# Normalisation rows fetched from sixteen DRAM copies, and a new order for the first two batches

## The chip, the cores and the metric

One Trainium2 chip; the program uses a single NeuronCore with its engines: PE (TensorE, matmuls), DVE (VectorE), ACT (ScalarE), POOL (GpSimd) and SP (SyncE, which here only issues DMAs). The metric is the device time of one execution in microseconds (us), less is better.

## The reference

One layer of a graph network over 64 batches of 256 tokens with 768 features:

```python
h = jnp.maximum(_layernorm(x, axis=-1), 0.0)
deg, rdeg = adj.sum(-1), swapaxes(adj, 1, 2).sum(-1)      # degrees, at least 1 where they divide
ctx = adj @ (h @ Wadj.T + badj) / deg + adj.T @ (h @ Wrev.T + brev) / rdeg + h @ Wself.T + bself
rel = agg @ Wr.T + br * deg + ragg @ Wrr.T + brr * rdeg   # agg, ragg: sums of rows of E over the neighbours
x = x + ctx + rel
```

All of it is float32. The adjacency matrix holds zeros and ones.

## The kernel before

The product of `h` (2 token tiles of 128, in 6 feature tiles) with the three weight matrices is made by a bilinear scheme of 15 products in place of 18 (`PRODUCTS`); every operand is split into two parts, so that three fast passes on PE give float32 accuracy. Batches 1 to 62 go twice through the chip: sweep 1 (8 of the products) for all of them, then sweep 2 (7 products and the multiplication with the adjacency matrix). What sweep 1 makes is stored to DRAM ("kept") and loaded again for sweep 2. Batch 0 and batch 63 don't use the scheme: `whole` multiplies them with the weights directly, in 144 slower matmuls each, while the prepared weights ("words", three for each product, made by POOL, ACT and DVE from the raw weights) are being made for the sweep that follows. So the order of time is: an opening with filler matmuls on PE ("early", "late", made by `idle`), batch 0 through `whole`, sweep 1 from about 65 us to 1,100 us, batch 63 through `whole`, sweep 2.

In front of each batch (`front1`) the layer norm's statistics are taken from `x`, token by token (one token is one partition). The products want `h` transposed, tokens along the free axis, so the mean and the power of the variance must be rows that every partition can read. For batches 1 to 63 the four columns of statistics (two token tiles, mean and scale) stand in `cols`, 8 floats apart; DVE's `transpose` turns them into `line`, in blocks of 32 by 32; SP stores them to a DRAM tile `d` (512 floats), waits for that store, and loads `d` into all 128 partitions as `row`; POOL subtracts the mean row from the transposed `x` (`centre`, tile `h`), DVE scales (`norm`). Batch 0 uses PE instead ("place" on ACT, "spread" on PE, then centre and norm on DVE). `x` is then added a bias row and stored to DRAM ("keep c01", in the trace `kept<-x`), which sets its buffer of class B free for the next operands ("left").

No engine's order is written by hand: `record` gives every operation a cost and a rank (base rank plus the entry of its kind in the table `OFFSETS`; never below the ranks of what it depends on), and `Plan.schedule` runs through time with those costs, takes on each engine the operation of lowest rank that could start, and so fixes each engine's program. SP's DMAs are issued in that order too; an SP instruction that must wait holds up those behind it. In the kinds, `@` marks batch 0, `@1` batch 1, `$1` and `$` batches 62 and 63; a kind without a mark is that of the other batches or of a shared operation. Buffers are slots of classes (`SLOTS`); `line` was one of six slots of class S.

By their ranks the first transfers of before are x1 (-2209), x0 (-1451), raw00 (-659), raw20 (-376), xt0 (-360), the bias row adj (-282), raw02 (-257), xt1 (-214), raw10 (-100). An x, an xt (transposed x of one token tile) and a bias row have 384 KB, a raw (a third of one weight matrix) 768 KB.

Of the kernel before, what the change touches and what calls it, by code (L numbers as in the profile page):

```python
# [10 lines left out]
F32 = mybir.dt.float32  # L11
# [3 lines left out]
ALU = mybir.AluOpType  # L15
AX = mybir.AxisListType

P = 128
# [64 lines left out]
AHEAD = 5.0  # L83
PACE = 5.0
# [17 lines left out]
    "b2-a1": -115.71, "b2-a1$1": -26.76, "b2-a1@1": 24.4, "bias adj": -308.49, "bias forward": 38.92,  # L102
    "bias rev": 8.51, "bias rev again": 15.38, "bias reverse": 37.66, "bias self": 29.13, "bias self again": 10.67,
# [10 lines left out]
    "degree": 7.82, "degree$": -107.61, "degree$1": -68.79, "degree@": -10.26, "degree@1": -1.22, "double adj": 37.35,  # L114
    "double own": 12.97, "eT": 9.08, "early@": 52.17, "eps": -95.99, "eps$": 0.14, "eps$1": -7.48, "eps@": 47.5,
# [8 lines left out]
    "first 8$1": -96.9, "first 8@1": 22.79, "first 9": 10.11, "first 9$1": 12.79, "first 9@1": 11.63, "flag": 294.89,  # L124
# [301 lines left out]
def record(nc, plan, fixed, B, NREL, part=None):  # L426
    F, C, H = 6, 2, 768
# [261 lines left out]
    def front1(b):  # L689
# [47 lines left out]
        else:  # L737
# [5 lines left out]
            def spread():  # L743
                nc.sync.dma_start(
                    t(d).rearrange("k (q j) -> q k j", q=4), t(line).rearrange("(m e) j -> m e j", e=8)[:, 0]
                )
# [518 lines left out]
```

## Time and profile before

| what | value |
|---|---|
| time, median of 3 runs | 2431.03 us (2430.84 to 2432.28) |
| the profiled execution, its own time | 2432.28 us |
| its span, first to last instruction | 2432.2 us |
| PE busy | 2414.3 us, 99% |
| DVE, ACT, POOL busy | 2111.8 (87%), 2083.9 (86%), 1413.5 us (58%) |
| granted PE clock, mean | 0.998 of full speed |
| DMA traffic | 593.06 MB, mean 244 GB/s |

PE's busy time counts pipelined matmuls with modelled ends, so a stretch can read as fully busy and still hold fewer matmuls than another of the same length. The number of matmuls in a stretch, the `x` count, tells more.

### The profile page before, as it was taken

The numbers are of one execution on the slowest core, as the hardware profiler recorded it, in microseconds if no ns is written. First come the engines' busy times: TensorE is split into PE (matmuls) and PEld (weight loads), VectorE is DVE, ScalarE is ACT, GpSimd is POOL, SyncE is SP. The second block draws the span as 40 slices with busy tenths as digits, with TensorE's granted clock in tenths as the row PEclk, the third lists the DMA queues.
The fourth block names the chain that finished last, engine by engine and source line by source line (L and its number), as shares of the span: only waits on it lengthen the run. The fifth ranks groups of instructions, "written<-read, shape, count | busy, mean of one in ns | idle before, by whom it ended". The sixth has DMA issues, their size and how long they took to land.

```text
span 2432.2 us, 43543 instructions
## 1 busy us (share of the span) xinstructions
PE 2414.3 (99%) x13600; PEld 2356.8 (97%) x13600; DVE 2111.8 (87%) x3953; ACT 2083.9 (86%) x3934; POOL 1413.5 (58%) x1230
## 2 busy tenths in 40 slices
PE   9999999999999999999999999999999999999998
PEld 6999999999999999996999999999999999999998
DVE  6888898888988988875888888898888888888988
ACT  7888888888888888887988888888888888888887
POOL 7666566666666666665555555555555555555554
PEclk9999999999999999999999999999999999999999
DMA  7788888888788888877666666666666666666664
GB/s 275 248 271 283 267 283 279 271 278 270 268 285 273 273 282 275 282 248 253 222 221 221 221 222 221 222 223 223 221 221 221 221 221 221 221 222 221 224 223 154
DMA packets 225545, 593.06 MB, mean 244 GB/s; under 512 B 25116, under 2 KB 25116, under 8 KB 225308
## 3 DMA queue, kind: packets, MB, share of 16 engines
q1 hardware_dynamic: 225308, 590.22, 71.8%
q8 instruction: 109, 1.79, 0.3%
q14 instruction: 128, 1.05, 0.1%
HBM read 366.65 MB, written 223.48 MB: 243 GB/s over the span
## 4 chain that ended last, share of the span: by engine, by line
PE 96%; ACT 1%; DVE 1%; DMA 1%; issue 1%; POOL 0%; SPq 0%; ACTq 0%; DVEq 0%; POOLq 0%
PE x L599 21%; PE y L599 20%; PE agg L936 14%; PE w L599 10%; PE z L599 10%; PE v L599 5%; PE t L599 5%; PE u L599 5%; PE whole L806 4%; DMA kept<-x 1%; PE spread L719 1%; ACT agg L944 0%; DMA kept_h<-h 0%; DVE c L681 0%; ACT y L652 0%
## 5 line engine op out<-in xcount | busy, mean ns | idle before, releaser
L924 POOL TENSOR_TENSOR hl<-c,hl 128x768 fp32r<-128x768 f32 x256 | 471.8, 1854 | 544.9 <-ACT hl L920 298.6
L599 PE MATMUL x<-word,left 128*128 128x384 f32 x2976 | 577.3, 335 | 1.3 <-ACT x L652 0.9
L599 PE MATMUL y<-word,left 128*128 128x384 f32 x2976 | 570.0, 335 | 2.1 <-DVE c L665 0.8
L599 PEld LDWEIGHTS y<-word,left 128*128 128x128 f32 x2976 | 519.4, 188 | 7.2 <-ACT y L652 3.2
L599 PEld LDWEIGHTS x<-word,left 128*128 128x128 f32 x2976 | 519.1, 188 | 4.6 <-ACT x L652 1.2
L936 PE MATMUL agg<-hl,a 128*128 128x384 f32 x2048 | 398.6, 336 | 3.7 <-ACT agg L944 3.7
L936 PEld LDWEIGHTS agg<-hl,a 128*128 128x128 f32 x2048 | 359.9, 188 | 5.2 <-ACT agg L944 4.5
L765 POOL TENSOR_TENSOR h<-h,row 128x768 f32<-128x768 f32 x126 | 231.4, 1856 | 216.9 <-DMA h<-in_x_t_dram 82.8
L599 PE MATMUL w<-word,left 128*128 128x384 f32 x1488 | 300.7, 336 | 1.0 <-ACT c L670 0.7
L599 PE MATMUL z<-word,left 128*128 128x384 f32 x1488 | 299.3, 335 | 0.2 <-ACT z L652 0.2
L599 PEld LDWEIGHTS w<-word,left 128*128 128x128 f32 x1488 | 260.7, 188 | 5.8 <-ACT c L670 3.4
L599 PEld LDWEIGHTS z<-word,left 128*128 128x128 f32 x1488 | 258.0, 188 | 4.3 <-ACT c L670 0.5
L954 DVE SCALAR_TENSOR_TENSOR c<-agg,rd,c 128x768 f32<-128x768 f32 x252 | 254.5, 1010 | 3.0 <-PE agg L936 2.1
L920 ACT ACTIVATE hl<-c 128x768 fp32r<-128x768 f32 x256 | 213.8, 836 | 0.7 <-DVE c L681 0.5
L652 ACT ACTIVATE x<-x 128x768 f32<-128x768 f32 x248 | 191.4, 793 | 26.0 <-PE x L599 18.4
L652 ACT ACTIVATE y<-y 128x768 f32<-128x768 f32 x248 | 195.3, 787 | 4.0 <-PE y L599 1.6
L588 DVE SCALAR_TENSOR_TENSOR left<-left,top 128x256 fp32r<-128x256 f32 x496 | 188.9, 411 | 0.3
L944 ACT ACTIVATE agg<-row_forward,sqd 128x768 f32<-128x768 f32 x128 | 115.4, 902 | 85.6 <-DVE c L679 85.6
L588 DVE SCALAR_TENSOR_TENSOR left<-left 128x256 fp32r<-128x256 f32 x434 | 185.4, 438 | 0.1
L578 ACT ACTIVATE top<-left 128x256 f32<-128x256 f32 x496 | 176.4, 381 | 9.8 <-DVE left L588 8.8
L681 DVE SCALAR_TENSOR_TENSOR c<-x,c 128x768 f32<-128x768 f32 x124 | 118.2, 953 | 68.8 <-ACT agg L944 66.1
L769 DVE SCALAR_TENSOR_TENSOR h<-h,row 128x768 f32<-128x768 f32 x126 | 149.2, 1186 | 0.0
(131 smaller groups left out, 4631.7 us busy)
## 6 DMA issues: line engine op xcount, KB each, us to landing
c<-kept SPq DMA_DIRECT2D x316, 384.0 KB
kept<-c SPq DMA_DIRECT2D x252, 384.0 KB
x<-in_x_dram SPq DMA_DIRECT2D x128, 384.0 KB
h<-in_x_t_dram SPq DMA_DIRECT2D x128, 384.0 KB
out_dram<-c SPq DMA_DIRECT2D x126, 384.0 KB
kept_h<-h SPq DMA_DIRECT2D x124, 384.0 KB
h<-kept_h SPq DMA_DIRECT2D x124, 384.0 KB
adj<-in_adj_dram SPq DMA_DIRECT2D x64, 512.0 KB
```

The source lines that it names most:

```text
L578: lambda: nc.scalar.activation(view(top), t(w)[:, 0].bitcast(F32), AF.Copy),
L588: lambda: nc.vector.scalar_tensor_tensor(t(w)[:, 2], t(w)[:, 1].bitcast(F32), -STEP, first(), op0=ALU.mult, op1=ALU.add), s == 1,
L599: nc.tensor.matmul(t(q)[:, half, : H // 2], t(w)[:, lw, f, :], t(r[rw])[:, f, ts(half, H // 2)], start=start and i == 0 and f == 0, stop=s ...
L652: lambda: nc.scalar.activation(view(), view(), AF.Copy, scale=scale),
L681: emit = lambda to=to, sign=sign: nc.vector.scalar_tensor_tensor(to(), view(), sign * UP, to(), op0=ALU.mult, op1=ALU.add)
L765: lambda h=h, one=one, engine=engine: engine.tensor_tensor(t(h), t(h), one(0), op=ALU.subtract),
L769: lambda h=h, one=one: nc.vector.scalar_tensor_tensor(t(h), t(h), 0.0, one(1), op0=ALU.max, op1=ALU.mult), b != 0 or part is not None,
L920: lambda: nc.scalar.activation(t(pair)[:, 0], t(o), AF.Copy, scale=LOWER),
L924: lambda: nc.gpsimd.tensor_tensor(t(pair)[:, 1], t(o), t(pair)[:, 0].bitcast(F32), op=ALU.subtract),
L936: nc.tensor.matmul(t(q)[:, half, : H // 2], t(s["a"])[:, c, k, ts(ic, P)], t(pairs[c])[:, part, ts(half, H // 2)], start=False, stop=(c == ...
L944: lambda q=q, ic=ic, row=row: nc.scalar.activation(t(q)[:, :, : H // 2], t(row).rearrange("p (k n) -> p k n", k=2), AF.Copy, scale=t(sqd)[ ...
L954: lambda q=q, to=to, ic=ic: nc.vector.scalar_tensor_tensor(to(), t(q)[:, :, : H // 2], t(rd)[:, ic, k : k + 1], to(), op0=ALU.mult, op1=AL ...
```

## The change

It has three parts.

1. `line` is one tile of 128 by 128 for the whole kernel instead of a slot for each batch. One transpose of 128 by 32 becomes four of 32 by 32, whose results stand side by side: `line` has the four statistics in partitions 0, 8, 16 and 24, 128 floats each. The planner's cost stays 0.17. (At the end `flag` uses the same tile for its scratch.)
2. `d` has sixteen copies of the 512 floats: the store writes 64 pieces of 512 bytes instead of 16 of 128, and `row` lets partitions 0 to 7 read the first copy, 8 to 15 the second, and so on. Before, all 128 partitions read the same 2 KB.
3. `OFFSETS` gets other entries for 216 kinds: those of batch 0 (57), batch 1 (95) and the words and loads of the opening; the entries of all other batches stay. `idle`'s counts of filler matmuls stay too.

```diff
+COPIES = 16
...
-            line = plan.buf("S", [P, 32], F32, f"line_{b}")
-            dve(0.17, r - 19.5, f"line {b}", [col], [line], lambda: nc.vector.transpose(t(line), t(col)))
-            d = plan.buf(None, None, None, "d", v["dram"].tile([4, P], F32, tag="d", name=f"d_{b}"))
+            line = v["line"]
+            def turn():
+                for q in range(4):
+                    nc.vector.transpose(t(line)[:32, ts(q, 32)], t(col)[ts(q, 32), :])
+            dve(0.17, r - 19.5, f"line {b}", [col], [line], turn)
+            d = plan.buf(None, None, None, "d", v["dram"].tile([COPIES, 4, P], F32, tag="d", name=f"d_{b}"))
...
-                    t(d).rearrange("k (q j) -> q k j", q=4), t(line).rearrange("(m e) j -> m e j", e=8)[:, 0]
+                    t(d).rearrange("r k p -> k r p"),
+                    t(line)[:32].rearrange("(k e) p -> k e p", e=8)[:, 0].unsqueeze(1).to_broadcast([4, COPIES, P]),
...
-                    t(row).rearrange("p k i -> p (k i)"), t(d).rearrange("k p -> (k p)").partition_broadcast(P)
+                    t(row).rearrange("p k i -> p (k i)"), t(d).rearrange("r k p -> r (k p)").unsqueeze(1).to_broadcast([COPIES, P // COPIES, 4 * P]),
...
-        rest = plan.buf("S", [P, B, C], F32, "rest")
+        rest = v["line"]
...
+            "line": own("line", [P, P], F32),
```

Of `OFFSETS`, the entries that the prediction speaks of, with the rank that follows (base rank plus entry) in brackets:

| kind | before | after |
|---|---|---|
| load raw00.0 | -673.18 (-659) | -1386.44 (-1372) |
| x1@, x0@ | -2208.17, -1448.79 (-2209, -1451) | -724.49, -711.01 (-725, -713) |
| load raw20.0 | -389.67 (-376) | -718.11 (-704) |
| xt1@ | -222.9 (-214) | -683.93 (-675) |
| load raw02.0 | -286.41 (-257) | -100.61 (-71) |
| bias adj | -308.49 (-282) | -96.49 (-70) |
| load raw10.0 | -113.7 (-100) | -23.35 (-9) |
| xt0@ | -367.66 (-360) | 15.05 (23) |
| write10@, write00@ | -1521.37, -590.36 (never below bias adj) | -37.41, 2.12 (-5, 27) |
| centre1@, centre0@ | -452.7, -6.79 | 44.54, 27.55 |
| early@, late@ | 52.17, 74.89 | 303.01, 51.7 |


## Rows read from the trace of the kernel before

**Rows 1.** The page, part 1: busy time, share of the span, instructions of each engine.

```profile
PE 2414.3 (99%) x13600; PEld 2356.8 (97%) x13600; DVE 2111.8 (87%) x3953; ACT 2083.9 (86%) x3934; POOL 1413.5 (58%) x1230
```

**Rows 2.** Windows of PE: length, PE busy (matmuls), granted clock, DMA share, GB/s.

```profile
100.00:1000.00 900.00, 899.38 (x5162) 1.00 0.83 276
1250.00:2150.00 900.00, 899.93 (x5184) 1.00 0.65 222
```

**Rows 3.** Timeline of PE, 0 to 80 us: start, length, what.

```profile
12.15 1.03 PE L732 MATMUL spread<-spread 128*128 128x256 f32 x4
13.02 2.17 PE L719 MATMUL spread<-ident 128*128 128x128 f32 x18
17.27 48.32 PE L806 MATMUL whole<-raw,h 128*128 128x384 f32 x144 [2.08 <-issue]
...
73.41 0.97 PE L599 MATMUL y<-word,left 128*128 128x384 f32 x4 [0.76 <-DVE c L665]
...
75.26 1.68 PE L599 MATMUL y<-word,left 128*128 128x384 f32 x8 [0.17 <-ACT y L652]
```

**Rows 4.** Windows of PE in the opening; the columns of rows 2.

```profile
65.60:75.30 9.70, 8.53 (x45) 1.00 0.65 230
```

**Rows 5.** Windows of the `whole` matmuls of batch 0 alone; the columns of rows 2.

```profile
17.27:21.77 4.50, 4.50 (x9) 0.63 1.03 401
21.77:65.70 43.93, 43.82 (x136) 1.00 0.71 250
```

**Rows 6.** Timelines of DVE, ACT and POOL, 0 to 32 us.

```profile
4.96 0.96 DVE L704 BATCH_NORM_STATS2 stats<-x 128x6 f32<-128x384 f32 x2
...
15.23 0.95 DVE L765 TENSOR_TENSOR h<-h,spread 128x768 f32<-128x768 f32 x1 [8.85 <-PE spread L719]
16.22 0.95 DVE L769 SCALAR_TENSOR_TENSOR h<-h,spread 128x768 f32<-128x768 f32 x1
...
7.27 0.98 ACT L726 ACTIVATE spread<-ident,cols 128x128 f32<-128x128 f32 x3 [0.60 <-POOL cols L712]
13.24 1.55 ACT L609 ACTIVATE whole<-row_adj 128x768 f32<-128x768 f32 x2 [4.98 <-DMA row_adj<-in_bias_dram]
...
11.08 3.58 POOL L497 TENSOR_TENSOR right<-raw,raw 128x768 f32<-128x768 f32 x2 [3.85 <-DMA raw<-in_Wadj_dram]
15.31 3.59 POOL L497 TENSOR_TENSOR right<-right,raw 128x768 f32<-128x768 f32 x2 [0.65 <-DMA raw<-in_Wrev_dram]
```

**Rows 7.** Windows of 1 us around one `row` load: length, clock, DMA share, GB/s.

```profile
246.34:247.34 1.00, 1.00 0.50 139
247.34:248.34 1.00, 1.00 0.98 98
248.34:249.34 1.00, 1.00 0.74 125
...
251.34:252.34 1.00, 1.00 1.05 406
```

**Rows 8.** The chain that ended last, 244 to 256 us: start, length, what.

```profile
246.70 6.62 DMA kept<-x
```

**Rows 9.** Timeline of ACT, 245 to 254 us.

```profile
253.40 0.42 ACT L571 ACTIVATE left<-a0+a1+b0+b 128x256 fp32r<-128x256 f32 x1 [0.72 <-DMA kept<-x]
```

**Rows 10.** Waits of SP, 100 to 1,000 us: total, times, longest.

```profile
SPq L751 <- DMA d<-line: 128.0, 52, 3.6
```

**Rows 11.** Timeline of SP, 500 to 545 us.

```profile
525.84 0.51 SPq L744 DMA_DIRECT2D d<-line  x1
...
530.37 0.32 SPq L751 DMA_DIRECT2D row<-d  x1
```

**Rows 12.** Timeline of DVE, 528 to 535 us.

```profile
530.66 0.20 DVE L739 STREAM_TRANSPOSE line<-cols 128x32 f32<-128x32 f32 x1
530.78 0.38 DVE L584 TENSOR_TENSOR left<-h,top 128x256 fp32r<-128x256 f32 x1
...
532.26 0.42 DVE L584 TENSOR_TENSOR left<-a1+b0+b,top 128x256 fp32r<-128x256 f32 x1 [0.43 <-ACT top L578]
```

More of the change, by code (lines that the diff above doesn't have):

```diff
@@ L99 @@
     "agg10$1": -0.91, "agg10@": -28.15, "agg10@1": -42.94, "agg11": -10.5, "agg11$": -53.27, "agg11$1": -82.29,
[2 rows of a table removed]
-    "b2-a1": -115.71, "b2-a1$1": -26.76, "b2-a1@1": 24.4, "bias adj": -308.49, "bias forward": 38.92,
-    "bias rev": 8.51, "bias rev again": 15.38, "bias reverse": 37.66, "bias self": 29.13, "bias self again": 10.67,
[10 rows of a table removed]
-    "degree": 7.82, "degree$": -107.61, "degree$1": -68.79, "degree@": -10.26, "degree@1": -1.22, "double adj": 37.35,
-    "double own": 12.97, "eT": 9.08, "early@": 52.17, "eps": -95.99, "eps$": 0.14, "eps$1": -7.48, "eps@": 47.5,
[7 rows of a table removed]
[2 rows of a table added]
+    "b2-a1": -115.71, "b2-a1$1": -26.76, "b2-a1@1": -93.81, "bias adj": -96.49, "bias forward": 38.92,
+    "bias rev": 30.12, "bias rev again": 15.38, "bias reverse": 37.66, "bias self": 39, "bias self again": 10.67,
[9 rows of a table added]
+    "degree$": -107.61, "degree$1": -68.79, "degree@": -10.26, "degree@1": -1.22, "double adj": 1.63,
+    "double own": 25.99, "eT": 9.08, "early@": 303.01, "eps": -95.99, "eps$": 0.14, "eps$1": -7.48, "eps@": -709.99,
[7 rows of a table added]
     "first 6@1": -30.97, "first 7": -34.24, "first 7$1": -134.25, "first 7@1": 13.92, "first 8": -22.36,
-    "first 8$1": -96.9, "first 8@1": 22.79, "first 9": 10.11, "first 9$1": 12.79, "first 9@1": 11.63, "flag": 294.89,
+    "first 8$1": -96.9, "first 8@1": -12.11, "first 9": 10.11, "first 9$1": 12.79, "first 9@1": 11.63, "flag": 294.89,
     "h0": -9.78, "h0$1": -10.44, "h0@1": 7.47, "h1": 4.83, "h1$1": 1.79, "h1@1": -8.6, "halve": -8.15, "high00": 1.38,
@@ L134 @@
     "init11$1": 135.32, "init11@": -10.65, "init11@1": 21.54, "keep c00": -90.11, "keep c00$1": -121.63,
[59 rows of a table removed]
-    "row@": -100.85, "row@1": -113.57, "rows": -60.11, "scale 1": -4.34, "scale 1$1": 60.81, "scale 10": -20.68,
[17 rows of a table removed]
-    "second 9$1": -175.69, "second 9@1": 18.85, "self less rev": -101.57, "spread0@": 1.75, "spread1@": -27.61,
-    "sqd": -3.42, "sqd$": -0.14, "sqd$1": 55.02, "sqd@": -59.31, "sqd@1": -25.66, "stats": 0.79, "stats$": 5.48,
[29 rows of a table removed]
[4 rows of a table added]
+    "keep h0$1": 47.05, "keep h0@1": 48.07, "keep h1": -95.74, "keep h1$1": 27.23, "keep h1@1": 44.31, "late@": 51.7,
[37 rows of a table added]
+    "pick": 33.09, "place0@": 55.73, "place1@": 48.57, "pow": -106.8, "pow$": -22.27, "pow$1": -269.06, "pow@": 58.18,
[8 rows of a table added]
+    "read 8$1": -15.51, "read 8@1": 31.47, "read 9": -0.79, "read 9$1": -16.16, "read 9@1": -58.25, "rest": -61.06,
[5 rows of a table added]
+    "rows": -60.11, "scale 1": -4.34, "scale 1$1": 60.81, "scale 10": -20.68, "scale 10$1": -413.44,
[17 rows of a table added]
+    "second 9@1": 18.85, "self less rev": 26.51, "spread0@": 63.59, "spread1@": 23.34, "sqd": -3.42, "sqd$": -0.14,
+    "sqd$1": 55.02, "sqd@": -59.31, "sqd@1": -25.66, "stats": 0.79, "stats$": 5.48, "stats$1": -11.07, "stats@": 20.36,
[28 rows of a table added]
 }
@@ L1005, in flag @@
         deg = v["deg"]
-        rest = plan.buf("S", [P, B, C], F32, "rest")
+        rest = v["line"]
+        pairs = lambda: t(rest).rearrange("p (b c) -> p b c", c=C)
         total = plan.buf("S", [P, 1], F32, "total")
@@ L1009, in flag @@
             0.4, start2[B - 2] + 1.0, "rest", [deg], [rest],
-            lambda: nc.vector.tensor_tensor(t(rest), t(deg)[:, :, :, 0], t(deg)[:, :, :, 1], op=ALU.subtract),
+            lambda: nc.vector.tensor_tensor(pairs(), t(deg)[:, :, :, 0], t(deg)[:, :, :, 1], op=ALU.subtract),
         )
-        dve(0.4, start2[B - 2] + 1.0, "total", [rest], [total], lambda: nc.vector.tensor_reduce(t(total), t(rest), AX.XY, ALU.add))
+        dve(0.4, start2[B - 2] + 1.0, "total", [rest], [total], lambda: nc.vector.tensor_reduce(t(total), pairs(), AX.XY, ALU.add))
         pf = plan.buf("Q", [P, 2, 512], F32, "pf")
```

249 rows, old and new, of the table OFFSETS are left out of this document.

## The prediction

> **What bounds the kernel now.** I read the page's busy times first: PE stands at 2414.3 of 2432.2 us, no other engine over 87% [rows 1]. So only time in which PE lacks work or runs slowly can be won, and everything that the change does on DVE, SP and the DMA engines counts only as far as PE feels it. Because busy matmuls are modelled, I then counted matmuls. Two windows of 900 us, one inside sweep 1 and one inside sweep 2, both read as fully busy, but sweep 1 holds 5162 matmuls and sweep 2 5184 [rows 2]. With 900/5184 = 0.1736 us as the dense pace, sweep 1 loses 22 x 0.1736 = 3.8 us in that stretch, in pieces too short to show as idle.
>
> The second look was at the opening. On PE the fillers and the two `spread` products end at 13.02 + 2.17 = 15.19, and `whole` starts at 17.27 after 2.08 us idle [rows 3]. Directly behind that idle time the granted clock falls: the window from 17.27 to 21.77 has 0.63 on average and 9 `whole` matmuls in 4.50 us, that is 0.50 us each, against 43.93/136 = 0.323 in the rest [rows 5], so part of it ran at 1.2 GHz instead of 2.4. All 144 at the rest's pace would take 46.5 us; they took 48.32 [rows 3]: 1.8 us lost. Behind `whole`, from 65.60 to 75.30, there are 45 matmuls, worth 45 x 0.1736 = 7.8 us, in 9.70 us: 1.9 us lost [rows 4], the longest single wait 0.76 us for DVE [rows 3]. Nothing before 75 us is hidden by anything else, so these pieces add up directly.
>
> **The row load.** One load of `row` (256 KB) fills about 3 us: the DMA engines are half to fully busy at 139, 98 and 125 GB/s, and three microseconds later they move 406 GB/s at the same busy share [rows 7]. So the single 2 KB source is what slows it. At 406 GB/s it would take 0.65 us, 2.3 us less. Who feels it: the store of `x`, issued right behind it, lands 6.62 us later [rows 8], ACT's next operand waits 0.72 us for the buffer which that store sets free [rows 9], and both stand on the chain that ended last. This is how a DMA reaches PE in a kernel that is bound by PE. With the load 2.3 us shorter the store would land before ACT asks. I book 3.0 of the 3.8 us lost in sweep 1, because I traced one such block only. Bounds: 0 (the other losses have another cause) and 3.8 (all).
>
> **The opening's new order.** By the new ranks SP's first transfers are raw00, x1, x0, raw20, xt1, raw02, the bias row, raw10, xt0. What an early place in the queue is worth I read from landings of before: 2304 KB had landed at 11.08, 3072 KB (through the bias row) at 13.24, 3840 KB at 15.31; both x's, 768 KB, by 4.96 [rows 6]. After, x0 ends at 1536 KB, halfway between 768 and 2304: about 8.0 us, 3 us later than before. From there to the end of "place" takes 7.27 + 0.98 - 4.96 = 3.3 us [rows 6], so `spread` could run at 11.3. It costs nothing, because the filler matmuls in front of `spread` hold PE until 12.15 [rows 3] and are as many as before; without that cover the 3 us would be lost. xt1 ends at 2688 KB, about 12.1. Then centre1 and norm1 (0.95 each) can follow the spread products at 13.2 and end at 15.1; if DVE waits for the late fillers as now (its centre starts at 15.23, 0.04 us behind them), they end at 17.1. The bias row ends at 3840 KB, 15.3, and ACT's write of the first bank takes half of 1.55: 16.1. So `whole` starts at 16.1 with batch 0's second token tile instead of 17.27 with its first: 1.2 us gained. Bounds: 0 (DVE waits for the fillers again) and 2.1 (straight behind them). raw10 is next in the queue and is needed 2.6 us after the start; xt0 is needed only after three such steps.
>
> PE's idle time ahead of `whole` then shrinks from 2.1 to 0.9 us. The wait of 0.76 us at 73 us left the clock at 1.00 [rows 3, 4], the one of 2.08 us did not. 0.9 is nearer to the first, so I book the whole 1.8 us of the slow clock. Bounds: 0 and 1.8.
>
> Behind `whole` PE would arrive 3 us earlier at products that it already waits for today [rows 4]. The same rights, words and operands must be made by then, in another order that I can't follow to the end by hand. I book nothing. Bounds: 1.9 gained (no waits left) and 3.0 lost (the first products come no sooner than now, so that both gains of the opening are eaten).
>
> **Four transposes and the shared tile.** One transpose takes 0.20 us and the next DVE instruction starts 0.12 us behind its start [rows 12]. Four take between 0.2 + 3 x 0.12 = 0.56 and 0.8 us: 0.36 to 0.6 us more for each of 63 batches, 23 to 38 us of DVE's time. Behind it DVE idles 0.43 us before its second next operand, waiting for ACT [rows 12], so the lower end is covered entirely and the upper end leaves 0.17 us, at most 62 x 0.17 = 10.5 us if every bit of it reached PE. A quarter of the work should not pitch slower than the whole does, so I stay near the lower end: 0.3 us lost.
>
> **The store of `d`.** It has 32 KB instead of 2. SP waits 128.0/52 = 2.5 us for it in each batch before it can issue `row`, with the loads of xt and x and the stores of x and c behind it [rows 10]. From issue to the `row` that waits for it 4.5 us pass [rows 11], mostly the queue ahead. At 406 GB/s 32 KB take 0.08 us; at a sixteenth of that, one engine's share, 1.3 us. I take 0.1, hidden by the 2.2 us that `row` saves right behind it. The Trainium skill speaks against this edit ("DMA: Bandwidth & Descriptors", Rules for kernel authors): a transfer whose outermost dimension is under 16 is confined to that many engines, and here that dimension is the four statistics. By that rule the store takes about 0.3 us, an estimate, and the sum would be the same less some tenths; the rows don't show how many engines it gets.
>
> **The sum.** 1.2 + 1.8 + 0 + 3.0 - 0.3 = 5.7 us, from the profiled execution's 2432.28: 2426.6. That execution was the slowest of three, 1.25 over the median; from the median 2431.03 the sum gives 2425.3, which is 0.23% faster. Differences under 0.2% (4.9 us, so times from 2426.2 to 2435.9) are about what a measurement of this kernel can't tell from no change, and my sum lies just past that edge.
>
> **Rivals.**
> - *The row load is hidden after all.* Sweep 1 keeps its 3.8 us, because the lost matmuls come from ACT and DVE being late in themselves; only the opening gains: 2431.0 - 2.7 = 2428.3. For it: PE's own idle time in sweep 1 is only 0.6 us [rows 2], and one traced block is thin. Against it: the store on the chain [rows 8].
> - *The opening gives its gain back* behind `whole`, where PE already waits: sweep 1 alone gains, 2431.0 - 2.7 = 2428.3.
> - *Everything works*: no waits behind `whole` either, all of sweep 1's losses and all the bounds of the opening: 2.1 + 1.8 + 1.9 + 3.8 = 9.6 us, 2421.4.
> - *Slower: DVE waits for the store.* With a single `line`, the transposes of a batch may overwrite it only when the store of the batch before has landed. In the batch shown the store had landed by 530.37 and the transpose started at 530.66 [rows 11, 12]: 0.29 us to spare, and 0.43 us of idle time behind it. It decides once the store and the three more transposes together cost over 0.72 us; with 0.6 for the transposes and 0.3 for the store they cost 0.9, and 62 x 0.18 = 11 us are lost on top of what the opening wins: 2431.0 - 2.7 + 11 = 2439. Against it: few batches are as tight, since SP's wait for the store is as a rule shorter than the 3.6 us of the worst [rows 10].
>
> **How the numbers follow.** The forecast has 45%, with a range of its own of 2422.5 to 2428; 36 of these lie past the edge. The hidden row load 20 (2 faster), the eaten opening 17 (2 faster), everything works 10, slower 8. Faster 0.50, same 0.42, slower 0.08. The range leaves out 2 in 10, the slow rival and the far end of the best one: 2420.5 to 2432.
>
> **What the profile after would show.** `whole` starts near 16.1 and no window behind it has a clock under 1; the window of 900 us in sweep 1 holds some 5180 matmuls; the 256 KB of `row` pass in under 1 us at about 400 GB/s and POOL's waits for `row` shrink; the transposes pitch at 0.12 us; SP's mean wait for `d` stays near 2.5 us. The prediction is wrong if the matmuls of sweep 1 stay at 5162 though `row` got fast, if PE waits longer behind `whole`, or if DVE shows waits for the store at the transposes.

## The result and the profile after

The change makes the kernel slower: 2450.91 us (2448.68 to 2452.45, 4 runs) against 2431.66 us (2430.84 to 2433.77, 4 runs) for the kernel before on the same chip. The ratio is 1.0077, with a 95% interval from 1.0065 to 1.009: 19.25 us lost, where 5.7 us gained were forecast. The profiled execution of the changed kernel took 2448.68 us, its span is 2446.9.

The page of the changed kernel, parts 1, 4 and 5 (in part 5: busy time, mean ns, then the idle time just before the group and what ended most of it):

```profile
PE 2424.9 (99%) x13600; PEld 2352.7 (96%) x13600; DVE 2135.4 (87%) x4142; ACT 2087.2 (85%) x3934; POOL 1414.8 (58%) x1230
...
PE 74%; DVE 10%; ACT 4%; issue 2%; DMA 1%; POOL 0%; SPq 0%; ACTq 0%; DVEq 0%
...
L596 PEld LDWEIGHTS y<-word,left 128*128 128x128 f32 x2976 | 517.6, 188 | 25.9 <-ACT y L649 22.1
...
L575 ACT ACTIVATE top<-left 128x256 f32<-128x256 f32 x496 | 178.3, 382 | 27.9 <-DVE left L585 27.2
```

The same three lines on the page of before, two of which I had not used:

```profile
PE 96%; ACT 1%; DVE 1%; DMA 1%; issue 1%; POOL 0%; SPq 0%; ACTq 0%; DVEq 0%; POOLq 0%
...
L599 PEld LDWEIGHTS y<-word,left 128*128 128x128 f32 x2976 | 519.4, 188 | 7.2 <-ACT y L652 3.2
...
L578 ACT ACTIVATE top<-left 128x256 f32<-128x256 f32 x496 | 176.4, 381 | 9.8 <-DVE left L588 8.8
```

PE's busy share is 99% as in [rows 1] and says nothing. The chain that ended last tells the story: it ran through PE for 96% of the span and now for 74%, with DVE at 10% and ACT at 4%. PE's weight loads of `y` wait 22.1 us for ACT's scale of `y` (before 3.2), and ACT's `top` waits 27.2 us for `left` on DVE (before 8.8).

Windows of PE in the changed kernel (length, busy and matmuls, granted clock, DMA share, GB/s):

```profile
100.00:1000.00 900.00, 894.56 (x5065) 1.00 0.81 272
1250.00:2150.00 900.00, 900.00 (x5187) 1.00 0.65 222
...
17.11:21.61 4.50, 4.50 (x14) 1.00 1.03 416
...
65.60:75.30 9.70, 9.34 (x53) 1.00 0.80 284
```

Against [rows 2], sweep 2 is as it was, and sweep 1 holds 97 matmuls fewer in 900 us: 97 x 0.1736 = 16.8 us. Sweep 1 goes on from 75 to about 1,095 us, so it loses 16.8 x 1020/900 = 19.1 us in all. In this execution the opening is ahead: 53 matmuls in the window that held 45 [rows 4], and 14 instead of 9 in the first 4.50 us of `whole` [rows 5], at full clock.

The opening on PE's timeline (start, length, what, idle time before and its releaser), where it can be laid beside [rows 3]:

```profile
11.67 1.03 PE L729 MATMUL spread<-spread 128*128 128x256 f32 x4
13.74 2.27 PE L716 MATMUL spread<-ident 128*128 128x128 f32 x18 [1.04 <-DVE h L768]
17.11 46.75 PE L809 MATMUL whole<-raw,h 128*128 128x384 f32 x144 [1.09 <-ACT word L514]
...
73.04 1.55 PE L596 MATMUL y<-word,left 128*128 128x384 f32 x8
```

`whole` starts at 17.11 instead of 17.27 and takes 46.75 us instead of 48.32. The matmuls of sweep 1 can be counted in both traces. The 100th starts at 82.1 us, before at 85.1: 3.0 us ahead. The 5,800th starts at 1,096.2, before at 1,080.1: 16.1 us behind. So 19.1 us are lost between the two, as the windows say, and 2432.28 + 19.1 - 3.0 = 2448.4, against 2448.68 for the profiled execution. (The two spans, 2432.2 and 2446.9, differ by less, 14.7 us.)

The 3.0 us are not shown to be the new order's. A kernel with the old `OFFSETS` (copies, below) has this on PE's timeline:

```profile
16.26 46.68 PE L807 MATMUL whole<-raw,h 128*128 128x384 f32 x144 [2.08 <-issue]
```

Its 100th matmul of sweep 1 starts at 82.1 as well. The profiled execution of before was late in its opening: `whole` began 1.0 us later than this and took 1.6 us more.

Now the place of the transposes. First DVE's timeline in one batch of the changed kernel, to be laid beside [rows 12]:

```profile
519.66 0.95 DVE L678 SCALAR_TENSOR_TENSOR x<-z,x 128x768 f32<-128x768 f32 x1
520.53 0.83 DVE L739 STREAM_TRANSPOSE line<-cols 32x32 f32<-32x32 f32 x4
521.39 0.42 DVE L581 TENSOR_TENSOR left<-h,top 128x256 fp32r<-128x256 f32 x1
521.73 0.74 DVE L585 SCALAR_TENSOR_TENSOR left<-left,top 128x256 fp32r<-128x256 f32 x2
522.66 0.42 DVE L581 TENSOR_TENSOR left<-a1+b0+b,top 128x256 fp32r<-128x256 f32 x1 [0.19 <-ACT top L575]
...
524.78 0.95 DVE L676 TENSOR_TENSOR c<-c,y 128x768 f32<-128x768 f32 x1 [0.71 <-PE y L596]
```

Then ACT's timeline of the same stretch:

```profile
520.98 0.81 ACT L606 ACTIVATE y<-row_adj 128x768 f32<-128x768 f32 x1
522.23 0.72 ACT L575 ACTIVATE top<-left 128x256 f32<-128x256 f32 x2 [0.45 <-DVE left L585]
522.89 0.77 ACT L649 ACTIVATE y<-y 128x768 f32<-128x768 f32 x1
```

From the start of the transposes to the next `left` 0.86 us pass, where it was 0.12 [rows 12]: 0.74 us later. Some of it is absorbed, for DVE's idle time before its second next operand shrinks from 0.43 to 0.19 us. But ACT's two `top` read what DVE makes right behind the transposes. They wait 0.45 us, and behind them in ACT's queue stands the scale of `y` that PE needs next.

### The profile page after: what moved, and what is told of

It reads as the page before. It is cut to its first block, busy times and chain, and to the rows that moved or that the text cites. A ratio compares the mean times of both kernels' runs of the same rounds, so it can differ in the third digit from the quotient of the medians.

```text
span 2446.9 us, 43766 instructions
## 1 busy us (share of the span) xinstructions
PE 2424.9 (99%) x13600; PEld 2352.7 (96%) x13600; DVE 2135.4 (87%) x4142; ACT 2087.2 (85%) x3934; POOL 1414.8 (58%) x1230
## 4 chain that ended last, share of the span: by engine, by line
PE 74%; DVE 10%; ACT 4%; issue 2%; DMA 1%; POOL 0%; SPq 0%; ACTq 0%; DVEq 0%
PE x L596 21%; PE agg L939 14%; PE y L596 12%; PE v L596 5%; PE t L596 5%; PE u L596 5%; PE z L596 5%; PE w L596 4%; DVE stats L701 2%; ACT top L575 2%; DVE left L585 2%; PE whole L809 2%; DVE left L581 2%; DVE x L678 2%; DVE line L739 1%
## 5 line engine op out<-in xcount | busy, mean ns | idle before, releaser
L596 PE MATMUL y<-word,left 128*128 128x384 f32 x2976 | 583.6, 337 | 5.5 <-ACT y L649 1.3
L596 PEld LDWEIGHTS y<-word,left 128*128 128x128 f32 x2976 | 517.6, 188 | 25.9 <-ACT y L649 22.1
L575 ACT ACTIVATE top<-left 128x256 f32<-128x256 f32 x496 | 178.3, 382 | 27.9 <-DVE left L585 27.2
L596 PE MATMUL v<-word,left 128*128 128x384 f32 x744 | 149.2, 334 | 0.0
```

The costliest lines, as they stand in the source:

```text
L575: lambda: nc.scalar.activation(view(top), t(w)[:, 0].bitcast(F32), AF.Copy),
L596: nc.tensor.matmul(t(q)[:, half, : H // 2], t(w)[:, lw, f, :], t(r[rw])[:, f, ts(half, H // 2)], start=start and i == 0 and f == 0, stop=s ...
```

## The experiments

Two theories: (1) the transposes delay DVE at that one place, and ACT carries the delay to PE; (2) the loss comes from elsewhere: waits of the shared `line` for its store, the larger store, or the new opening. Each experiment was timed alternately with the kernel before, whose median was 2431.0, 2431.15 and 2431.92 us in the three sets. "Period" is the median distance from the transposes of one batch to those of the next in sweep 1, worked out from the trace. It is 16.648 us before and 17.027 after, 0.38 us more. The median leaves out the few longer batches; the mean between 100 and 1,000 us is 16.745 before and 17.076 after, 0.33 us more. 19.1 us over some 60 batches are 0.32 us each, so where the text prices a batch, it goes by the mean or by the time.

| experiment | median us | ratio to before, 95% | period us | matmuls 100 to 1000 us |
|---|---|---|---|---|
| after | 2450.91 | 1.0077 [1.0065, 1.009] | 17.027 | 5065 |
| turns | 2465.06 | 1.0142 [1.0125, 1.0159] | 17.046 | 5038 |
| copies | 2431.26 | 1.0002 [0.9993, 1.0012] | 16.648 | 5166 |
| opening | 2439.68 | 1.0039 [1.0025, 1.0053] | 16.657 | 5153 |
| copies and opening | 2435.45 | 1.0014 [1.0004, 1.0024] | 16.679 | 5148 |
| one copy | 2452.41 | 1.0087 [1.007, 1.0103] | 17.034 | 5047 |
| turns and copies | 2460.88 | 1.0124 [1.0107, 1.0141] | 17.045 | 5056 |
| moved | 2429.18 | 0.9991 [0.9982, 1.0001] | 16.650 | 5161 |
| moved, one copy | 2433.63 | 1.001 [1.0001, 1.002] | 16.678 | 5148 |
| dose 2 | 2434.34 | 1.0012 [1.0002, 1.0021] | 16.679 | 5145 |
| dose 3 | 2440.44 | 1.0032 [1.0021, 1.0044] | 16.767 | 5122 |
| dose 4 | 2450.52 | 1.0077 [1.006, 1.0094] | 16.994 | 5081 |
| told | 2434.12 | 1.0008 [0.9998, 1.0018] | 16.648 | 5177 |

**The parts alone.** The first four kernels take the change apart: the transposes and the shared `line` alone (after, with the old `OFFSETS` and one copy); the copies alone; the new `OFFSETS` alone in the kernel before; copies and `OFFSETS` together. The store of copies writes its 32 KB in 256 pieces of 128 bytes, not in 64 of 512.

```diff
 turns:    after, with OFFSETS of before and
-COPIES = 16
+COPIES = 1
 copies:   before, with the 16 copies written from the old line
-... v["dram"].tile([4, P], F32, tag="d", name=f"d_{b}"))
+... v["dram"].tile([16, 16, 32], F32, tag="d", name=f"d_{b}"))
-    t(d).rearrange("k (q j) -> q k j", q=4), t(line).rearrange("(m e) j -> m e j", e=8)[:, 0]
+    t(d).rearrange("r m j -> m r j"),
+    t(line).rearrange("(m e) j -> m e j", e=8)[:, 0].unsqueeze(1).to_broadcast([16, 16, 32]),
-    ... t(d).rearrange("k p -> (k p)").partition_broadcast(P)
+    ... t(d).rearrange("r m j -> r (m j)").unsqueeze(1).to_broadcast([16, P // 16, 4 * P])
 opening:  before, with OFFSETS of after
 copies_opening:  both edits
```

> The changed kernel with one copy of the rows and the ranks of before, so that of the three parts only the four transposes and the shared tile are left. Theory 1 (the four transposes stand in a loop of PE, DVE and ACT with about 0.36 us of slack per batch, and what is over goes into the time): a batch of sweep 1 takes 17.0 us instead of 16.65, some 60 of them +22 us: 2450 to 2456 us. Theory 2 (the store of 32 KB holds SP up, or DVE waits for it): with 2 KB the loss is mostly gone, 2431 to 2438. Theory 3 (the new ranks lead the planner into a slower steady order): no loss, 2429 to 2434.

> The kernel before with sixteen copies of the rows, stored from its own 128 by 32 transpose; the four statistics then stand in another order inside a row, so the normalisation uses the wrong tokens' rows, at the same cost. Theory 1: no loss, and if the slow load of rows was what PE felt in sweep 1, up to 3.8 us gained: 2427.5 to 2432. Theory 2: slower, 2440 to 2455, since the store of 32 KB is in it. Theory 3: as before, 2429 to 2433.

> The kernel before with the new ranks alone. Theory 1: the opening's gain alone, 2.2 us by the first dense stretch of PE (73.04 after, 75.26 before) : 2428 to 2431. Theory 2: the same. Theory 3: the whole loss, 2448 to 2453.

> Sixteen copies and the new ranks with the single transpose of before (statistics in another order, as in the run with copies alone). Theory 1: the sum of both parts' gains, 2424 to 2430, faster than before. Theory 2: slower than before through the store, 2440 to 2455. Theory 3: slower than before through the ranks, 2446 to 2453.

Only the kernel with the new transposes has the long period, so they, with the shared `line`, carry the loss of sweep 1, and neither the copies nor the new opening does. But turns, opening and copies with opening all came out in none of the ranges expected. Alone, the transposes lose 34 us, not 19: the opening suffers too. In that kernel the DVE timeline has

```profile
54.38 0.83 DVE L743 STREAM_TRANSPOSE line<-cols 32x32 f32<-32x32 f32 x4
...
57.12 0.87 DVE L743 STREAM_TRANSPOSE line<-cols 32x32 f32<-32x32 f32 x4
...
61.57 0.89 DVE L743 STREAM_TRANSPOSE line<-cols 32x32 f32<-32x32 f32 x4
```

and PE's timeline and windows:

```profile
68.17 3.27 PE L600 MATMUL w<-word,left 128*128 128x384 f32 x8 [5.14 <-ACT left L572]
...
62.00:82.00 20.00, 12.94 (x50) 0.78 0.64 226
```

In the kernel before the transposes of batches 1 and 2 stand together at 44.86 us. With one shared tile batch 2's start at 57.12, 2.7 us behind batch 1's, and the chain that ended last leads from them to that wait of PE:

```profile
58.02 2.00 DMA d<-line
60.02 0.02 issue
60.04 0.49 SPq L758
60.53 0.05 issue
60.58 5.19 DMA x<-in_x_dram
```

SP waits for the second store of `d` before it can issue `row`, and a load of `x` stands behind that in its queue. The granted clock of the stretch is 0.78. The 50 matmuls between 62 and 82 us were 95 in the kernel before: 45 x 0.1736 = 7.8 us. (Four repeats of the old transpose with a slot of `line` for each batch, dose 4 below, hold 85 there.) Why the first transposes themselves moved from 44.86 to 54.38 I did not separate. The new `OFFSETS` take most of this back: in the changed kernel the three sets stand at 42.85, 45.91 and 51.24 us. By themselves they cost 8.7 us on the kernel before and 4.2 with the copies. Their profiled execution, the fastest of the five, shows 2 us of that in its span; where the rest lies is open.

The row load got as fast as forecast: by the packets of the trace, the loads between 100 and 1,000 us (54 before, 52 after) took from first to last packet 3.6 us in the median before and 1.3 us after. The profile of copies alone shows 5166 matmuls in sweep 1's window, 4 more than before, and its time is that of before.

**Copies against the slow kernel.** Next the copies were taken from the changed kernel, and the ranks from it alone:

```diff
 one_copy:
-COPIES = 16
+COPIES = 1
 turns_copies:  after, with OFFSETS of before
```

> The changed kernel with one copy of the rows instead of sixteen: four transposes, shared tile and new ranks. The runs so far gave +34 us for the transposes with the shared tile, 0 for the copies, +8.7 for the ranks, and +19 for all three, so the parts don't add. If the new ranks are what takes back the loss that the shared tile makes in the opening (5.3 and 1.9 us of waiting on PE there with the old ranks), this run is near the changed kernel, 2449 to 2455. If it is the copies that take it back, it is slower, 2460 to 2470.

> The changed kernel with the ranks of before: four transposes, shared tile, sixteen copies. If the ranks take the opening's loss back, this run keeps it: 2460 to 2468. If the copies take it back: 2449 to 2455.

With one copy the changed kernel takes 1.5 us more (the intervals overlap), and turns takes 4.2 us less with sixteen. So the larger store is no part of the loss.

**The dose.** If DVE's time at that place is what counts, the kernel before must lose by repeating its one transpose there:

```diff
-... lambda: nc.vector.transpose(t(line), t(col)))
+... lambda: [nc.vector.transpose(t(line), t(col)) for _ in range(2)])   # 3 in dose3, 4 in dose4
```

> The kernel before with its one transpose done twice, the second with the same result; nothing else. One more costs 0.21 us of DVE at the same place. Theory 1 (0.36 us of slack, then one for one): nothing, 2429 to 2433, batches of 16.65 us. Rival (each added DVE time costs its share, 0.38 of 0.74): 60 x 0.11 = 6.5 us, 2436 to 2439, batches of 16.76 us.

> The kernel before with its one transpose done three times at the same place. A repeat costs DVE 0.25 us, by the run with two (0.37 us from the first transpose to the next instruction, 0.12 with one). Theory 1 (slack of 0.3 to 0.36 us, then one for one): 0.50 us more, 0.17 us over, batches of 16.82 us, 2438 to 2445. Rival (each added microsecond of DVE costs the same share from the first on, 3.2 us for one repeat): 2437 to 2438, batches of 16.71 us.

> The kernel before with its one transpose done four times: DVE's added time is that of the changed kernel, but each batch keeps its own tile and the ranks are the old ones. Theory 1: batches of 17.0 to 17.1 us, 2450 to 2458, of which the opening takes little; the 12 us that the run with four transposes and the old ranks lost on top of this came from the single shared tile, whose next write must wait for the store. Rival (the time in the opening came from the longer transposes themselves): 2463 to 2467, like that run.

DVE's timeline in the dose of two shows the price of one more, 0.37 - 0.12 = 0.25 us:

```profile
514.33 0.44 DVE L739 STREAM_TRANSPOSE line<-cols 128x32 f32<-128x32 f32 x2
514.70 0.38 DVE L584 TENSOR_TENSOR left<-h,top 128x256 fp32r<-128x256 f32 x1
```

For 0.25, 0.50 and 0.75 us more on DVE the times grow by 3.2, 8.5 and 18.6 us, or 0.05, 0.14 and 0.30 us for each of 62 batches: about a fifth of the first repeat is paid and two thirds of the last. (The median periods grow by 0.03, 0.12 and 0.35 us.) So slack and then one for one, which I had expected, is too sharp; dose 2 lies between my two theories, doses 3 and 4 in the range of the first. Four repeats in the kernel before, with its old store, its own slots for `line` and its old ranks, lose nearly as much as the change does. Counted from the 100th to the 5,800th matmul it is 16.1 us in sweep 1, where the change loses 19.1; what makes the other 3 I did not separate. The wait for the store is not the main cause in sweep 1; in the changed kernel the view of `line` shows such waits only twice:

```profile
L739 DVE STREAM_TRANSPOSE line<-cols x252: 188/199/205, 42.8 to 1095.0; 32x32 f32<-32x32 f32 x126
...
  DMA d<-line: 0.6, 2
```

The dose of two has the old opening, and on PE the same wait of 2.08 us ahead of `whole` as in [rows 3], but `whole` at full speed behind it, with a granted clock of 1.00 in its first 4.50 us:

```profile
16.17 46.68 PE L806 MATMUL whole<-raw,h 128*128 128x384 f32 x144 [2.08 <-issue]
```

Copies shows the same. So the partly half-clocked start of `whole` in the profile of before belongs to that execution, not to the code.

**The place.** The changed kernel, with the transposes of batches 4 to 60 moved in DVE's order behind the next seven DVE instructions, where DVE waits 0.71 us for PE in the timeline above (the edit in short):

```diff
+for o in [o for o in order if o.name.startswith("line ") and 4 <= int(o.name[5:]) <= 60]:
+    i = j = order.index(o); n = 0
+    while n < 7:
+        j += 1; n += order[j].eng == "DVE"
+    order.insert(j + 1, o); del order[i]
```

> The changed kernel, with the four transposes of batches 4 to 60 moved behind the next seven DVE instructions, to where DVE waits 0.71 us for PE; the same instructions otherwise. Theory 1 (what counts is the place: the transposes stand in the loop from DVE through ACT to PE, with 0.36 us of slack): a batch takes 16.65 us again, 57 x 0.38 = 22 us come back: 2427 to 2433. Rival (DVE's added time counts wherever it stands, because DVE is the pace of sweep 1): 17.03 us, 2449 to 2453.

> The run with the moved transposes, with one copy of the rows instead of sixteen. With DVE out of the way it shows what the sixteen copies are worth in a sweep that PE bounds. If the slow load of rows is hidden: within 2 us of the moved run, 2427 to 2432. If PE feels it, as the prediction booked: 3 us slower than the moved run or more, 2432 to 2436.

DVE's timeline in moved:

```profile
513.89 0.75 DVE L585 SCALAR_TENSOR_TENSOR left<-left,top 128x256 fp32r<-128x256 f32 x2
514.55 0.84 DVE L739 STREAM_TRANSPOSE line<-cols 32x32 f32<-32x32 f32 x4
515.48 0.95 DVE L676 TENSOR_TENSOR c<-c,y 128x768 f32<-128x768 f32 x1
```

The transposes take as long as in the changed kernel, now in what was idle time: `c` follows without a wait. ACT still does its two `top` (512.75) ahead of the scale of `y` (513.36), and neither waits. The period is back at 16.650, and the kernel takes 2429.18 us. That is 22 us less than after, and not to be told from before. The single `line`, the sixteen copies and the new `OFFSETS` are all still in it, so none of them is a cause in sweep 1 by itself. With one copy it takes 4.45 us more, so here the faster row load is worth something.

**The cost that the plan is told.** The changed kernel still gives the planner 0.17 us for work that takes 0.83:

```diff
-dve(0.17, r - 19.5, f"line {b}", [col], [line], turn)
+dve(0.85, r - 19.5, f"line {b}", [col], [line], turn)
```

> The changed kernel, with the planner told that the transposes take 0.85 us instead of 0.17. In the steady part of sweep 1 the planner still puts them behind the same read of z. Theory 1 (the place decides): batches of 17.0 us, 2446 to 2454. Rival (the loss is an error of the plan, which a right cost mends): 16.65 us, 2427 to 2433.

I had expected the loss to stay, and was wrong: 2434.12 us, period 16.648, the most matmuls of all in sweep 1. The transposes are where they were in DVE's order and still take 0.83 us. Its time lies 5 us over that of moved, since the new cost changes the opening too: between 62 and 82 us PE has 87 matmuls in told and 106 in moved, 19 x 0.1736 = 3.3 us. What matters here is ACT's timeline:

```profile
516.01 0.81 ACT L606 ACTIVATE y<-row_adj 128x768 f32<-128x768 f32 x1
516.74 0.78 ACT L649 ACTIVATE y<-y 128x768 f32<-128x768 f32 x1
517.43 0.69 ACT L575 ACTIVATE top<-left 128x256 f32<-128x256 f32 x2
```

The scale of `y` now goes ahead of the two `top`, so it no longer waits for DVE. In the usual batch of sweep 1 this swap is the only difference: the orders of DVE, PE, POOL and SP are those of the changed kernel. On PE it shows in one run of twelve matmuls of `y`, first in the changed kernel, then in told:

```profile
522.09 2.58 PE L596 MATMUL y<-word,left 128*128 128x384 f32 x12
...
517.12 2.24 PE L596 MATMUL y<-word,left 128*128 128x384 f32 x12
```

Those are 0.34 us for the same work, which PE's busy time doesn't show as idle. Theory 1 thus needs its second half: it is ACT's order, `top` before the scale, that passes DVE's delay to PE. Take away the delay (moved) or change the order (told), and the loss of sweep 1 is gone.

## Why the prediction was wrong

**The step that failed is "Four transposes and the shared tile"**: booked at 0.3 us lost, measured at about 19 in sweep 1. First the size. I took a pitch of 0.12 us because the next instruction starts 0.12 us behind a transpose [rows 12], but that one is of another kind. Four transposes take 0.83 us and start 0.21 us apart, with nothing overlapped; the whole one, repeated, costs 0.25 us each time (dose 2), so 0.12 was never the pitch of transposes. The next instruction comes 0.74 us later, not 0.36 to 0.6, and I had booked the step near the lower end of even that.

Then the cover. I read the 0.43 us of idle time behind it [rows 12] as hiding a delay up to that length and passing the rest on. In amount this was close: with the measured delay my own sum gives 0.74 - 0.43 = 0.31 us, and 62 x 0.31 = 19.2 us. As a mechanism it was wrong, so that agreement is partly luck. The doses show no such edge: 0.25 us more, well under 0.43, already cost 3.2 us. DVE's idle time itself keeps 0.19 of its 0.43 us. The instructions between the transposes and that idle time are late, and ACT waits for them, with the scale of `y` in its queue behind. I asked who waits for DVE only at DVE's next idle time, not at the first result behind the transposes. The page had a hint: ACT's `top` already waited 8.8 us in all for that kind of `left`.

**The slow rival** ("DVE waits for the store") named the right engine and place and the wrong mechanism for sweep 1: two waits of 0.6 us in all. The serial use of one `line` does show in the opening under the old ranks (turns). No rival had ACT's queue in it.

**The row load.** Right in its rate (3.6 to 1.3 us; forecast 2.3 us less, measured 2.3), wrong in what it is worth on the kernel before: 0, where 3.0 us were booked. In the kernels with the new transposes or ranks sixteen copies are worth 1.5 to 4.5 us. My sign that POOL's waits for `row` would shrink did not come; between 100 and 1,000 us they grew from 39.5 us in 11 waits to 66.1 in 27, while its waits for the transposed `x` fell from 75.8 to 20.6. The rival "the row load is hidden after all" is the better reading for the kernel before.

**The opening.** `whole` came at 17.11, not 16.1. The fillers in front of it themselves wait 1.04 us for DVE's centre, whose place between the products of `spread` and the fillers I had not seen. DVE's norm, which `whole` needs, then waits for the fillers:

```profile
16.05 0.95 DVE L772 SCALAR_TENSOR_TENSOR h<-h,spread 128x768 f32<-128x768 f32 x1 [2.37 <-PE spread L716]
```

This is the case that I had priced at 0. So the 1.2 us shrank to 0.2, and against the 16.26 of copies, with the old order, `whole` is 0.9 us late. The clock term of 1.8 us came in this execution, but copies and dose 2 show that it was never the code's to give. Behind `whole`, where I booked nothing, 8 x 0.1736 = 1.4 us came back against the profile of before, and 0.9 us against that of copies, just what was lost ahead of `whole`.

**The store of `d`** cost no time that the runs show. SP's waits for it went from 128.0/52 = 2.5 us [rows 10] to 2.3 us each, but the transposes changed with it. With the same transposes 32 KB cost more than 2 KB: 2.3 against 107.3/51 = 2.1 us with one copy, and 131.8/52 = 2.5 against 111.8/51 = 2.2 us in the two kernels with moved transposes. The lines of the changed kernel and of one copy:

```profile
SPq L754 <- DMA d<-line: 121.2, 52, 3.7
...
SPq L754 <- DMA d<-line: 107.3, 51, 3.6
```

By these waits the store takes some 0.2 to 0.3 us more, not the 0.1 that I took, and `row` saves more than that right behind it. The Trainium skill's rule ("DMA: Bandwidth & Descriptors", Rules for kernel authors), that an outermost dimension under 16 leaves a transfer to that many engines, isn't contradicted by this: the estimate of 0.3 us from it is near what was measured. No run here shows how many engines the store got.

The range ended at 2432 because the only case with a loss at that place had 8 in 100, and even it ended at 2439.

## What to carry to other kernels

When an edit makes an instruction longer on an engine that isn't the bound, follow the first result behind it, not that engine's next idle time: whoever waits for that result has a queue of its own, and what the bound engine needs may stand in it. A planner's cost belongs to the edit: an operation of 0.83 us booked at 0.17 made an order that loses 0.3 us per batch, and the right figure, or a place in true idle time, gave that back. Test such a place by dose: here about a fifth of the first quarter of a microsecond was paid, and two thirds of the third. And before a gain is read from two profiles, look at a third: of the 3.0 us by which the opening seems to win, 2.6 are the lateness of one execution.

## What the runs showed of the hardware

- A transpose of 32 by 32 takes as long as one of 128 by 32 (0.20 us), and transposes of 32 by 32 in a row don't overlap: 0.21 us from start to start, while a tensor-tensor operation started 0.12 us behind one.
- 128 partitions reading the same 2 KB of DRAM took 3.6 us in the median; the same 256 KB from sixteen copies took 1.3 us.
- The clock behind the same idle time is not fixed by the code: after 2.08 us of it, `whole` had a granted clock of 0.63 in its first 4.50 us and took 48.32 us in the execution of before; in those of copies and dose 2 it had 1.00 there and took 46.68.
